# Idle matmuls during the first load, earlier and later places for statistics, more value buffers, and a different end of the program

## The chip, the cores and the metric

The kernel runs on one core of one Trainium2 chip. It is one program and one launch. The metric is the device time of that launch in microseconds, lower is better; a kernel is run several times and the median is given. One further execution is recorded by the hardware profiler; its times are what the profile shows.

## The reference, cut to what matters

Four images of 56 x 56 positions with 256 channels, in f32, pass through four layers. Each layer normalises its input by groups of channels (32 groups of 8, over the whole image), does its own mixing and adds the result to its input:

```python
def _gn(v, G=32, eps=1e-5):
    g = v.reshape(B_, H_, W_, G, C_ // G)
    m = jnp.mean(g, axis=(1, 2, 4), keepdims=True)
    s = jnp.var(g, axis=(1, 2, 4), keepdims=True)
    return ((g - m) / jnp.sqrt(s + eps)).reshape(v.shape)

x = x + L0(_gn(x))   # 7x7 local attention, 8 heads of 32, zero padding
x = x + L1(_gn(x))   # every position against all 3136 of its image
x = x + L2(_gn(x))   # 7x7 neighbourhood attention, 4 heads at dilation 1, 4 at dilation 2
x = x + L3(_gn(x))   # shifted 7x7 windows, 8 heads
```

Layers 0, 2 and 3 are attention: three projections of 256 x 256 to queries, keys and values, logits plus a bias or mask, softmax, the products with the values, and an output projection. Layer 1 normalises rows to unit length, computes exp(5(A - max A)) of all inner products A without the diagonal, divides by the row sums, and applies a 256 x 256 matrix, a norm over channels and a leaky relu to the difference between the row and its weighted mean.

Since the statistics of a group cover a whole image, no row of an image can enter a layer before the last row of that image has left the layer before.

## The kernel before, in words

**Engines.** TensorE (PE) does all products, VectorE (DVE) reciprocals, mask additions and the writing of results with a residual, ScalarE (ACT) exponentials and copies with a bias, GpSimd (POOL) the multiplication of exponentials by masks and the sums of pairs. SyncE (SP) issues nearly all transfers, in one queue of instructions: an issue that has to wait holds up every later one. Each engine runs its instructions in the order in which the program gives them. A planner may choose the order within layers; `issue_after(x)` places what is inside it behind the instruction x in the engine's order. For layer 3 the order is that of the text (`manual_schedule` for PE, DVE, ACT and POOL), for layer 1 that of PE and DVE.

**Layers one after the other.** `direct_blocks` (line 831 on) runs layers 0 to 3. The residual stream goes through DRAM from layer to layer. An image is cut into 7 pieces of 448 positions in layer 0, 8 of 392 in layers 2 and 3. The next layer's first loads and weights are brought in while the layer before ends (`layer2_ahead`, `layer3_ahead`).

**Statistics.** `add_stats` (L896) runs `bn_stats` on DVE for each piece. When the last piece of an image is in, three steps are put into a list `pending`: `channels` (DVE, L910), `mean` (one matmul with a matrix that averages over groups, L914, then ACT, L916 and L917) and `scale` (two matmuls, L921 and L922, then ACT L923 and POOL L924 to L928). `step_stats` takes the next step off the list, `known` takes all that are needed. The matmuls of the steps that run between units write into four spare columns of the bank in which that unit's products lie (`spare`).

**Units.** In layers 0 and 2 the work is a chain of units, each a pair of tiles of queries for 8 heads (`attend_pairs`, L1055 on). For a unit, PE computes the logits (L1080), DVE adds a mask to half of them (L1087), ACT takes exponentials (L1088, L1090), and POOL multiplies the other half by the exponential of the mask (L1091) and adds pairs (`both`, L1102). The products with the values and the row sums (L1113) come one unit later, behind the next unit's logits and a number of "fill" steps (projections of later rows: L952 for queries, keys and outputs, L981 for values). After the products, the unit's list "after" takes steps of statistics, and `done` divides by the row sums (DVE L1272, L1275, L1277 in layer 0; L2008, L2012 in layer 2). In layer 0 a row has four units; `then` (L1329) says which of them take a step of statistics.

**The first image.** Seven pieces are loaded (L1167, order 3, 4, 5, 6, 0, 1, 2); each goes to `bn_stats`; then `known(0, 0)` takes the three steps, ACT normalises (L942), and L981 makes the first values.

**Layer 2.** 16 rows of 8 units (4 images of 4 rows; grids m = 0, 1; pairs i = 0 to 3). Before a unit's logits `gather` (L1990) issues four to eight transfers on SP (L2002), which bring the values of the neighbourhood out of DRAM (`vd`) into a tile `vp2`, of which there are three. `project_out` (L2032) multiplies a finished row by the output weights, adds the residual on DVE (L2044) and stores it. In the last rows `layer3_ahead` is woven in: it loads the first pieces of layer 3, its weights `w_qkv3` in three transfers (L2166) and a mask `m3a` (L2205), normalises two rows, and makes their values.

**Layer 3.** Before its stream of units, layer 3 normalises its third row: `prepare(2)` (L2346), six DVE instructions L945, placed behind `newest[0]`, at that time the last mask addition L1087 of layer 2. The load of the fourth row is issued by `prepare(2)` too.

**The end.** The last row's projection is added to the residual by DVE (`last_row`, L2322) and stored. Throughout, sums which would show an overflow are collected in four tiles `watch`. `unsafe` (L2421) reduces each of them (L2428, four instructions behind `last`, the last addition), compares them to a bound, sums over partitions with a matmul and writes a flag. Every engine loads the flag (L2506) and branches (L2507): if it were set, the whole would be computed again in a slower, safe way (`fused_blocks`); with these inputs it never is, and the branch goes past that code to the closing semaphores and drains.

Of the kernel before, what the change touches and what calls it, by code (L numbers as in the profile page):

```python
# [24 lines left out]
FP = mybir.dt.float32  # L25
# [6 lines left out]
NIMG = 4  # L32
# [798 lines left out]
def direct_blocks(ctx: ExitStack, tc: tile.TileContext, d: dict, watch):  # L831
# [57 lines left out]
    stats, pending, spare = {}, [], []  # L889
# [11 lines left out]
    def group_stats(l, b):  # L901
# [10 lines left out]
        def mean():  # L912
            pm = spare[0](0) if spare else ps_m()
            nc.tensor.matmul(pm[:, :CC], lhsT=group, rhs=mv[:, :, 0], start=True, stop=True)  # L914
# [4 lines left out]
        def scale():  # L919
            pm = spare[0](1) if spare else ps_m()  # L920
            nc.tensor.matmul(pm[:, :CC], lhsT=group, rhs=dv, start=True, stop=False)  # L921
            nc.tensor.matmul(pm[:, :CC], lhsT=group, rhs=mv[:, :, 1], start=False, stop=True)  # L922
# [235 lines left out]
    def layer0(early, big, pool, begin_layer1):  # L1158
# [16 lines left out]
        for r in (3, 4, 5, 6, 0, 1, 2):  # L1175
            load(r, *(() if r < 3 else (looks, "xs")))
            if r < 3:
                add_stats(0, 0, r, xs[r])
            else:
                first_look(r)  # L1180
        known(0, 0)
# [127 lines left out]
        def stream():  # L1309
# [10 lines left out]
            for r in range(NIMG * NB0):  # L1320
# [8 lines left out]
                then = [int(i < 3 and (g > 2 or g == 0)) for i in range(NTC)]  # L1329
# [122 lines left out]
    def layer1(early, big, pool, first, late, next_layer):  # L1452
# [12 lines left out]
        def look_up(q):  # L1465
            if q % 7 == 0:
                rows[:] = [pool.tile([98, 7, NH], FP, tag="rows", name="rows", bufs=1)]
            with tc.issue_after(scaling[-1].ins):
                nc.gpsimd.indirect_dma_start(out=rows[0][:, q % 7, :], out_offset=None, in_=d["table"][:, :],
                                             in_offset=bass.IndirectOffsetOnAxis(ap=idx[:, q:q + 1], axis=0))  # L1470
# [406 lines left out]
    def layer2_ahead(early, held):  # L1877

        xs = held["xs"] = {}

# [17 lines left out]
    def layer2(held, big, pool, last_steps, ends, begin_layer3):  # L1898
# [66 lines left out]
        def pair(r, m, i):  # L1965
# [24 lines left out]
            def gather():  # L1990
                box["o"] = psum_tile("o", 2)
                box["v"] = pool.tile([P, 2, 2, P], FP, tag="vp", name="vp2", bufs=3)
# [41 lines left out]
        def project_out(r):  # L2034
            b, g = divmod(r, NSB)

            def step(y, m, box={}):
# [6 lines left out]
                nc.vector.scalar_tensor_tensor(x[:, m, :], pm, bp2[:, m:m + 1], x[:, m, :], ALU.add, ALU.add)  # L2044
# [99 lines left out]
    def layer3_ahead(big, early, own):  # L2144
# [21 lines left out]
        def load_weight(k):  # L2166
            nc.sync.dma_start(out=w_qkv[:, :, k * C:(k + 1) * C],
                              in_=d["wqkv3"].rearrange("(h p) o -> p h o", p=P)[:, :, k * C:(k + 1) * C])
# [35 lines left out]
        def load_mask():  # L2204
            nc.sync.dma_start(out=m3, in_=m3d[:, 0, :4].rearrange("p h w k -> p h (w k)"))  # L2205

        steps = [lambda: (load(0), load_weight(2)), lambda: load_weight(1),
                 lambda: (prepare(0, later), load_weight(0)), lambda: (prepare(1, later), load_mask())]
        return [transfer, xns, vd, m3, w_qkv, parts, prepare], steps, lazily(values, 0, 3) + lazily(values, 1, 3)

    def layer3(front, pool):
# [152 lines left out]
        u4["done"]()  # L2364
        first()
# [52 lines left out]
    return newest[0].ins  # L2418


def unsafe(tc, pool, watch, flag, last):  # L2421

    nc = tc.nc
    n = len(watch)
    t = pool.tile([P, n + 2], FP, name="bounds")
# [94 lines left out]
```

## Time and profile before

| | us |
|---|---|
| runs shown: median (lowest, highest) of 3 | 3722.86 (3720.98, 3726.05) |
| the profiled execution's own time | 3720.84 |
| its span in the trace | 3719.0 |
| TensorE busy | 3645.2 |
| VectorE busy | 2197.2 |
| GpSimd busy | 1802.9 |
| ScalarE busy | 1479.4 |

The mean granted clock of TensorE is 0.996. In the profile, L12 means line 12 of the kernel; an instruction is written as output tile, line, what it reads and its size; behind it stands the idle time of the engine just before, with the instruction that ended it. A matmul of f32 data appears as two records. Matmuls are pipelined, so busy time counts the engine as taken and not at its peak: at half the clock it is just as busy. In tables of windows there follow, for each stretch, its length, the busy time (and the number of instructions) of PE, weight loads, DVE, ACT and POOL, the granted clock, the busy share of the transfer engines, and GB/s.

### The profile page before, as it was taken

What the parts mean: (1) busy time and instruction counts of PE and PEld (TensorE: products, weight loads), DVE (VectorE), ACT (ScalarE), POOL (GpSimd) and SP (SyncE); (2) the same over time, 40 slices, a digit from 0 to 9 for tenths busy, and PEclk for the clock granted to TensorE, in tenths of its full rate; (3) what the DMA queues carried; (4) which work ended last, traced back from release to release, by engine and by line L of the source; (5) the groups of instructions that cost most, each with busy time, mean ns of one, the idle gap of its engine ahead of it and who ended that gap; (6) DMA issues with size and microseconds to landing.
All of it is one profiled execution on the core that took longest, in us unless ns stands there. A gap on an engine that the chain in (4) does not pass through costs nothing.

```text
span 3719.0 us, 112489 instructions
## 1 busy us (share of the span) xinstructions
PE 3645.2 (98%) x48938; PEld 2480.5 (67%) x48938; DVE 2197.2 (59%) x4176; ACT 1479.4 (40%) x3137; POOL 1802.9 (48%) x1952
## 2 busy tenths in 40 slices
PE   8999999999999999999999999999999999999998
PEld 4666666677776777767777777776666666555554
DVE  5787777544445444554444643445777777677776
ACT  5666665422222222222222222223666666444443
POOL 4777777421235222352222521124877778455555
PEclk9999999999999999999999999999999999999999
DMA  6554444300011000100000000002455444544443
GB/s 223 167 162 138 142 127 139 112 7 24 23 29 33 18 19 19 30 28 23 19 19 23 28 15 11 11 20 78 121 139 145 135 135 127 157 135 133 132 133 100
DMA packets 278695, 304.95 MB, mean 82 GB/s; under 512 B 33670, under 2 KB 269578, under 8 KB 277838
## 3 DMA queue, kind: packets, MB, share of 16 engines
q1 hardware_dynamic: 276336, 297.43, 26.6%
q8 instruction: 386, 6.32, 0.7%
q0 software_dynamic: 1568, 0.16, 0.1%
q14 instruction: 117, 0.96, 0.1%
q10 hardware_dynamic: 288, 0.08, 0.0%
HBM read 205.04 MB, written 92.55 MB: 80 GB/s over the span
## 4 chain that ended last, share of the span: by engine, by line
PE 90%; DVE 4%; POOL 1%; DMA 1%; issue 1%; ACT 1%; SPq 0%; DVEq 0%; ACTq 0%; POOLq 0%
PE ps_m L952 19%; PE ps_o L1683 14%; PE ps_s L1561 14%; PE ps_v L1688 13%; PE ps_m L981 7%; PE ps_o L1113 6%; PE ps_s L1080 6%; PE ps_t L1669 3%; PE ps_o L1040 2%; PE ps_s L1024 1%; PE ps_m L1526 1%; DMA vp<-vd 1%; POOL b L1102 1%; PE ps_m L1418 1%; PE ps_m L1754 1%
## 5 line engine op out<-in xcount | busy, mean ns | idle before, releaser
L1593 DVE TENSOR_TENSOR acc<-acc,ps_v 128x257 f32<-128x257 f32 x1088 | 457.5, 422 | 774.8 <-PE ps_v L1688 751.8
L1688 PE MATMUL ps_v<-xw,e 128*128 128x257 f32 x2208 | 611.1, 381 | 3.5 <-DVE xnT L1538 2.2
L1683 PE MATMUL ps_o<-xw,at 128*128 128x257 f32 x2208 | 609.0, 379 | 0.0
L1561 PE MATMUL ps_s<-xnT,xd 128*128 128x512 f32 (+3 forms) x1344 | 571.4, 548 | 3.9 <-DVE xnT L1538 3.9
L1672 ACT COPY at<-ps_t 128x512 f32<-128x512 f32 (+3 forms) x332 | 170.4, 513 | 953.6 <-PE ps_t L1669 953.4
L1688 PEld LDWEIGHTS ps_v<-xw,e 128*128 128x128 f32 x2208 | 413.4, 189 | 145.0 <-issue 83.2
L1102 POOL TENSOR_TENSOR b<-e 124x448 f32<-124x448 f32 (+5 forms) x498 | 484.7, 994 | 7.2 <-PE ps_o L1113 0.3
L1683 PEld LDWEIGHTS ps_o<-xw,at 128*128 128x128 f32 x2208 | 419.1, 190 | 60.1
L952 PE MATMUL ps_m<-xn,w_wqkv 128*32 128x392 f32 x4096 | 374.3, 494 | 2.3 <-PE ps_s L1080 1.1
L1554 POOL TENSOR_SCALAR xd<-xnT,vec 128x128 f32<-128x128 f32 x192 | 116.1, 614 | 475.6 <-PE ps_s L1561 475.4
L1564 ACT ACTIVATE e<-ps_s 128x512 f32<-128x512 f32 x336 | 185.3, 552 | 354.4 <-PE ps_s L1561 351.1
L1561 PEld LDWEIGHTS ps_s<-xnT,xd 128*128 128x128 f32 x1344 | 225.4, 191 | 141.4 <-issue 126.2
L1091 POOL TENSOR_TENSOR e<-e,m0t 126x672 f32<-126x672 f32 (+3 forms) x128 | 238.7, 1865 | 158.6 <-ACT e L1090 126.2
L1091 POOL TENSOR_TENSOR e<-e,bias 119x784 f32<-119x784 f32 (+5 forms) x128 | 241.7, 1888 | 151.6 <-ACT e L1090 150.8
L1113 PEld LDWEIGHTS ps_o<-e,vp 124*32 124x32 f32 (+3 forms) x8192 | 198.0, 110 | 104.4 <-issue 85.3
L1002 ACT ACTIVATE no<-rs 128x168 f32<-128x168 f32 (+2 forms) x256 | 93.9, 367 | 385.8 <-DVE rs L2008 185.9
L952 PEld LDWEIGHTS ps_m<-xn,w_wqkv 128*32 128x32 f32 x4096 | 124.3, 109 | 176.5 <-issue 128.7
L2008 DVE RECIPROCAL rs<-ps_o 128x196 f32<-128x196 f32 (+2 forms) x128 | 175.7, 1373 | 103.6 <-PE ps_o L1113 83.4
L1113 PE MATMUL ps_o<-e,vp 124*32 124x112 f32 (+3 forms) x8192 | 227.6, 248 | 4.2 <-DMA vp<-vd 3.9
L1088 ACT ACTIVATE e<-e 126x672 f32<-126x672 f32 (+5 forms) x256 | 219.6, 858 | 17.4 <-DVE e L1087 5.0
L1090 ACT ACTIVATE e<-ps_s 126x672 f32<-126x672 f32 (+5 forms) x256 | 206.1, 805 | 8.6 <-PE ps_s L1080 6.4
L981 PE MATMUL ps_m<-w_wqkv,xn 128*32 128x256 f32 x3136 | 197.6, 381 | 3.8 <-DVE xr L2044 2.0
(235 smaller groups left out, 5973.6 us busy)
## 6 DMA issues: line engine op xcount, KB each, us to landing
x<-xr SPq DMA_DIRECT2D x64, 392.0 KB
x<-in_x SPq DMA_DIRECT2D x53, 448.0 KB
x<-x SPq DMA_DIRECT2D x60, 392.0 KB
xr<-x SPq DMA_DIRECT2D x60, 392.0 KB
vd<-v SPq DMA_DIRECT2D x72, 256.0 KB
xr<-in_x SPq DMA_DIRECT2D x32, 392.0 KB
xr<-x SPq DMA_DIRECT2D x28, 448.0 KB
x<-xr SPq DMA_DIRECT2D x28, 448.0 KB
```

The lines of the kernel that those rows point to most:

```text
L952: nc.tensor.matmul(pm[j * HD:(j + 1) * HD, :n], lhsT=w[:, h, col + j * HD:col + (j + 1) * HD], rhs=rhs(h), start=(h == 0), stop=(h == CC - 1))
L981: nc.tensor.matmul(pm[i:i + HD, j * C:(j + 1) * C], lhsT=xn[:, h, first + i:first + i + HD], rhs=w[:, h, :], start=(h == 0), stop=(h == CC ...
L1080: nc.tensor.matmul(s[j // 2][:nk, j % 2, (2 * i + u) * nq:(2 * i + u + 1) * nq], lhsT=k(j, u), rhs=q(j), start=True, stop=True)
L1088: newest.append(nc.scalar.activation(ev, ev, AF.Exp))
L1090: nc.scalar.activation(ev, sv, AF.Exp)
L1091: nc.gpsimd.tensor_tensor(parts(ev), parts(ev), w["emask"], ALU.mult)
L1102: nc.gpsimd.tensor_tensor(w["b"][a][:nk, :, :2 * nq].rearrange("p h (i c) -> p h i c", i=2), ev[:, :, :, 0, :], ev[:, :, :, 1, :], ALU.add)
L1113: nc.tensor.matmul(w["o"](k, i)[j * HD:(j + 1) * HD], lhsT=ones[:nk, :HD] if k else v(j, u), rhs=w["b"][j // 2][:nk, j % 2, i * nq:(i + 1) ...
L1561: nc.tensor.matmul(s[:, :n], lhsT=xd[j][:, h, :], rhs=xnT[:, h, first * P:last * P], start=(h == 0), stop=(h == CC - 1))
L1593: nc.vector.tensor_tensor(acc[:, i, :], acc[:, i, :], pv[:, :C + 1], ALU.add)
L1683: nc.tensor.matmul(out[j][:, :C + 1], lhsT=e[:, col(i)] if i == j else at[:, col(i)], rhs=xw[:, i, :], start=(i == j), stop=(i == NB - 1))
L1688: nc.tensor.matmul(pv[:, :C + 1], lhsT=e[:, col(i)], rhs=xw[:, j, :], start=True, stop=True)
```

## The change

It has five parts.

1. While the pieces of the first image arrive, TensorE multiplies them with an identity matrix, after each load so many times as the tuple (0, 2, 2, 2, 2, 1, 0) says, nine in all, 128 x 448 each; the result is read by nobody. Three more follow the statistics' last matmul. The statistics' steps are placed behind these matmuls in TensorE's order (`grouped`).
2. In layer 0, a row's units 1, 2 and 3 take a step of statistics each, instead of units 0, 1 and 2.
3. In layer 2's last two rows, five units gather their values into tiles of the pool that held layer 2's input pieces ("x", two of them), not into one of the three `vp2`. The three transfers of layer 3's weights become one, and it and the mask are issued by ACT, behind the newest exponential, instead of SP.
4. `newest[0]` becomes the last addition L2044 in the last row of layer 2, so that `prepare(2)` is placed behind it.
5. At the end three of the four reductions of `watch` come before the last row's first half; the fourth stays last, in a block of its own which begins with a hint, on all engines, that the branch over the safe version will be taken. In layer 1, GpSimd executes a drain behind the last of its 49 gathers from a table (L1469).

```diff
+        def busy(x, n):
+            pm = psum_tile("s0", 1, 2)
+            for i in range(n):
+                grouped[:] = [nc.tensor.matmul(pm[:, i % 2, :CH], lhsT=ident, rhs=x[:, i % 2, :], start=True, stop=True)]
+
+        for i, r in enumerate((3, 4, 5, 6, 0, 1, 2)):
             load(r, *(() if r < 3 else (looks, "xs")))
+            busy((xs if r < 3 else looks)[r], (0, 2, 2, 2, 2, 1, 0)[i])
...
-        known(0, 0)
+        for _ in range(3):
+            with tc.issue_after(grouped[0].ins):
+                pending.pop(0)()
+        with tc.issue_after(grouped[0].ins):
+            busy(xs[0], 3)
...
-                then = [int(i < 3 and (g > 2 or g == 0)) for i in range(NTC)]
+                then = [int(i > 0 and (g > 2 or g == 0)) for i in range(NTC)]
...
+            if q == WN - 1:
+                with tc.issue_after(got.ins):
+                    nc.gpsimd.drain()
...
-                box["v"] = pool.tile([P, 2, 2, P], FP, tag="vp", name="vp2", bufs=3)
+                if r < NIMG * NSB - 2 or (8 * r + 2 * i + m) % 5 < 3:
+                    box["v"] = pool.tile([P, 2, 2, P], FP, tag="vp", name="vp2", bufs=3)
+                else:
+                    x = held["pool"].tile([P, CC, WC2], FP, tag="x", name="vx2").rearrange("p h t -> p (h t)")
+                    box["v"] = x[:, :4 * P].rearrange("p (t u e) -> p t u e", t=2, u=2)
...
-                nc.vector.scalar_tensor_tensor(x[:, m, :], pm, bp2[:, m:m + 1], x[:, m, :], ALU.add, ALU.add)
+                added = nc.vector.scalar_tensor_tensor(x[:, m, :], pm, bp2[:, m:m + 1], x[:, m, :], ALU.add, ALU.add)
+                if r == NIMG * NSB - 1:
+                    newest[0] = added
...
-        def load_weight(k):
-            nc.sync.dma_start(out=w_qkv[:, :, k * C:(k + 1) * C],
-                              in_=d["wqkv3"].rearrange("(h p) o -> p h o", p=P)[:, :, k * C:(k + 1) * C])
+        def load_weight():
+            with tc.issue_after(newest[1].ins):
+                nc.scalar.dma_start(out=w_qkv, in_=d["wqkv3"].rearrange("(h p) o -> p h o", p=P))
...
         def load_mask():
-            nc.sync.dma_start(out=m3, in_=m3d[:, 0, :4].rearrange("p h w k -> p h (w k)"))
-
-        steps = [lambda: (load(0), load_weight(2)), lambda: load_weight(1),
-                 lambda: (prepare(0, later), load_weight(0)), lambda: (prepare(1, later), load_mask())]
+            with tc.issue_after(newest[1].ins):
+                nc.scalar.dma_start(out=m3, in_=m3d[:, 0, :4].rearrange("p h w k -> p h (w k)"))
+
+        steps = [lambda: load(0), load_weight, lambda: prepare(0, later), lambda: (prepare(1, later), load_mask())]
...
+        for i in (1, 3, 2):
+            add_up_watch(i)
         first()
         second()
...
-                last = direct_blocks(tc, d, watch)
-                unsafe(tc, wp, watch, flag, last)
+                n = len(watch)
+                bounds = wp.tile([P, n + 2], FP, name="bounds")
+                nc.vector.memset(bounds[:, n + 1:], 1.0)
+
+                def add_up_watch(i):
+                    nc.vector.tensor_reduce(bounds[:, i:i + 1], watch[i], AX.X, ALU.add)
+
+                direct_blocks(tc, d, watch, add_up_watch)
+                with tc.block():
+                    tc.mark_branch_hint_location("again", hint="LikelyTaken", engines=list(mybir.ALL_ENGINES))
+                    add_up_watch(0)
+                    unsafe(tc, bounds, n, flag)
             again = nc.values_load(flag)
-            with tc.If(again > 0):
+            with tc.If(again > 0, label="again"):
                 fused_blocks(tc, d)
```

More of the change, by code (lines that the diff above doesn't have):

```diff
@@ L830, in direct_blocks @@
 @with_exitstack
-def direct_blocks(ctx: ExitStack, tc: tile.TileContext, d: dict, watch):
+def direct_blocks(ctx: ExitStack, tc: tile.TileContext, d: dict, watch, add_up_watch):
     nc = tc.nc
@@ L888, in direct_blocks @@
     raw = [[const.tile([P, CC, n, 6], FP, name=f"st{l}_{b}") for b in range(NIMG)] for l, n in enumerate(parts_of)]
-    stats, pending, spare = {}, [], []
+    stats, pending, spare, grouped = {}, [], [], []
     seen_parts = {}
@@ L913, in mean @@
             pm = spare[0](0) if spare else ps_m()
-            nc.tensor.matmul(pm[:, :CC], lhsT=group, rhs=mv[:, :, 0], start=True, stop=True)
+            grouped[:] = [nc.tensor.matmul(pm[:, :CC], lhsT=group, rhs=mv[:, :, 0], start=True, stop=True)]
             for h in range(CC):
@@ L921, in scale @@
             nc.tensor.matmul(pm[:, :CC], lhsT=group, rhs=dv, start=True, stop=False)
-            nc.tensor.matmul(pm[:, :CC], lhsT=group, rhs=mv[:, :, 1], start=False, stop=True)
+            grouped[:] = [nc.tensor.matmul(pm[:, :CC], lhsT=group, rhs=mv[:, :, 1], start=False, stop=True)]
             nc.scalar.activation(dv, pm[:, :CC], AF.Identity, bias=gn_eps)
@@ L1174, in layer0 @@
         q = {(0, i): early.tile([P, CC, BT], FP, tag="q", name="q0", bufs=6) for i in range(3)}
-        for r in (3, 4, 5, 6, 0, 1, 2):
+        def busy(x, n):
[3 more added lines that the diff above has]
+        for i, r in enumerate((3, 4, 5, 6, 0, 1, 2)):
             load(r, *(() if r < 3 else (looks, "xs")))
+            busy((xs if r < 3 else looks)[r], (0, 2, 2, 2, 2, 1, 0)[i])
             if r < 3:
@@ L1468, in look_up @@
             with tc.issue_after(scaling[-1].ins):
-                nc.gpsimd.indirect_dma_start(out=rows[0][:, q % 7, :], out_offset=None, in_=d["table"][:, :],
-                                             in_offset=bass.IndirectOffsetOnAxis(ap=idx[:, q:q + 1], axis=0))
+                got = nc.gpsimd.indirect_dma_start(out=rows[0][:, q % 7, :], out_offset=None, in_=d["table"][:, :],
+                                                   in_offset=bass.IndirectOffsetOnAxis(ap=idx[:, q:q + 1], axis=0))
+            if q == WN - 1:
+                with tc.issue_after(got.ins):
+                    nc.gpsimd.drain()
             if q % 7 == 6:
@@ L1879, in layer2_ahead @@
         xs = held["xs"] = {}
+        held["pool"] = early
         def load(i):
@@ L2417, in direct_blocks, with unsafe @@
     fronts.close()
-    return newest[0].ins
-def unsafe(tc, pool, watch, flag, last):
+def unsafe(tc, t, n, flag):
     nc = tc.nc
-    n = len(watch)
-    t = pool.tile([P, n + 2], FP, name="bounds")
-    for i, w in enumerate(watch):
-        with tc.issue_after(last):
-            nc.vector.tensor_reduce(t[:, i:i + 1], w, AX.X, ALU.add)
     nc.vector.tensor_tensor(t[:, :n], t[:, :n], t[:, :n], ALU.mult)
@@ L2431, in unsafe @@
     nc.vector.tensor_reduce(t[:, n:n + 1], t[:, :n], AX.X, ALU.min)
-    nc.vector.memset(t[:, n + 1:], 1.0)
     with tc.tile_pool(name="psum_end", bufs=1, space=PSUM) as ps:
```

## The prediction

> **What bounds the kernel now.** I read the busy table and the chain first, then asked where TensorE's remainder lies.
>
> ```profile
> PE 3645.2 (98%) x48938; PEld 2480.5 (67%) x48938; DVE 2197.2 (59%) x4176; ACT 1479.4 (40%) x3137; POOL 1802.9 (48%) x1952
> PE 90%; DVE 4%; POOL 1%; DMA 1%; issue 1%; ACT 1%; SPq 0%; DVEq 0%; ACTq 0%; POOLq 0%
> ```
>
> TensorE is busy for 3645.2 of 3719.0 us. The change removes no matmul of the computation, so it can only fill the 74 us left over, or turn half-clock time, which counts as busy, into full-clock time. The timeline of the start shows the first place:
>
> ```profile
> 4.89 1.15 DVE L896 BATCH_NORM_STATS2 st<-x 128x6 f32<-128x448 f32 x2 [0.62 <-DMA x<-in_x]
> 13.98 0.59 PE L914 MATMUL ps_m<-mv,group 128*128 128x2 f32 x2 [13.98 <-DVE mv L910]
> 18.71 5.35 PE L981 MATMUL ps_m<-w_wv,xn 128*32 128x256 f32 x48 [2.62 <-ACT xn L942]
> ```
>
> TensorE waits 13.98 us for seven loads and the statistics on DVE. The 48 matmuls of L981 then take 5.35 us; the same 48 take 2.6 us late in the run (379 ns each instead of 634). So the start runs at half clock, although the granted-clock column, which has its first record at 24.67, cannot say so.
>
> The waits of TensorE, asked stretch by stretch (us in total, times, longest), show three more places: layer 0 (127 to 135 us), the end of layer 2 (3143 to 3200), and the passage to layer 3 (3200 to 3215).
>
> ```profile
> PE ps_m L952 <- DVE attn L1277: 0.8, 1, 0.8
> ...
> PE ps_o L1113 <- DMA vp<-vd: 3.6, 6, 1.0
> ...
> PE ps_m L981 <- DVE xr L2044: 2.0, 1, 2.0
> ```
>
> Each of the latter two is followed by half clock. In the windows below, read the first pair (TensorE's busy time) and the sixth figure (granted clock):
>
> ```profile
> 3171.77:3175.18 3.41, 1.56 (x36) 0.68 (x28) 2.11 (x4) 2.02 (x4) 3.41 (x4) 1.00 0.55 181
> 3175.18:3178.59 3.41, 3.14 (x60) 2.48 (x58) 1.30 (x1) 0.00 (x0) 1.17 (x1) 0.50 0.42 140
> 3202.49:3205.90 3.41, 1.37 (x40) 0.94 (x40) 3.41 (x7) 0.00 (x0) 0.93 (x1) 1.00 0.12 45
> 3205.90:3209.31 3.41, 3.41 (x68) 2.50 (x60) 2.96 (x6) 0.44 (x2) 0.00 (x0) 0.50 0.59 195
> ```
>
> Last, the end. DVE's flag is done at 3709.57, the span ends at 3719.0: 9.5 us in which no engine computes. The sequencers' records there: loads of the flag to 3710.1, compare-and-branch to 3710.29, nothing on any engine until 3713.8 to 3714.35, SP's row of semaphores to 3715.45, GpSimd's DRAIN 3714.14 to 3718.21 (4069 ns; its other three drains take 172, 106 and 40 ns), a barrier of 0.84.
>
> **Part by part.**
>
> *A, multiplications during the load.* Nine 128x448 matmuls enter before L914, three after L922. No row has them; the nearest is L1561 (512 columns, 571.4 us / 1344 = 425 ns per record, two records each), so 0.74 us warm and 1.49 cold. The first has its image rows at about 6.2. Records of the clock lie on a grid of 3.413 us through 24.67, so the first wholly busy window would be 7.60 to 11.02. Until 11.02 3.2 are done, the other 5.8 take 4.3: L914 starts at 15.3 instead of 13.98, 1.3 late (1.49 us each throughout would end at 19.6, 5.6 late). The three statistics matmuls, warm (0.38 against 0.59 for L914; 0.61 against 1.02 for L921 with L922), return 0.6. The three later ones take 2.2 us and lie inside the 2.6 us wait for ACT's normalisation. L981 then saves 2.7. Net with the clock up: 2.0; if the half clock returns before L981, a loss of 0.7. [...] the row 13.98 says that the warm-up itself stands in the queue ahead of L914. I take 1.0, between, range -1.8 to +2.7.
>
> *B, statistics in layer 0.* Steps that fell on a row's first unit now fall on the unit before it in TensorE's order (L914 or L921/L922 one unit or one row earlier). At 285.3 ACT's L916/L917 read the bank which DVE's L1272 wants (1.24 us wait), the mask addition L1087 goes ahead of L1277, and L952 waits: 0.77 at 130.33, 0.97 at 288.89, 0.97 at 447.98, sum 2.7. A longer wait at 622.52 (0.88) stays. Nothing becomes later. DVE's 0.53 for L910 lies behind a unit of matmuls. 2.7 (1.5 to 3).
>
> *C, value buffers.* In rows 14 and 15 five units (m is the grid, i the pair) use tiles left free by the loads, so their gathers L2002 need not wait until a buffer of three is read; three loads of weights (0.64, 0.71, 0.47) and the mask (0.45) leave SP, 2.27 us, with the lane waits behind them:
>
> ```profile
> SPq L2041 <- DMA x<-xr: 1.5, 1, 1.5
> SPq L2002 <- DMA m3a<-m3d: 1.1, 1, 1.1
> ```
>
> Units take 3.52 us undisturbed; three of them in 3161 to 3184 take 2.2, 3.05 and 2.9 more: 8.2 us, of which 3.56 are the waits above and 3.4 the half clock of 3175.18 to 3182.00 (6.8 / 2); the rest is pauses between. SP issues 4 to 8 gathers of 0.73 us per unit, and GpSimd's multiplications and sums (L1091, L1102) stand behind as the next bound:
>
> ```profile
> 3143.00:3161.00 18.00, 17.69 (x468) 12.09 (x462) 15.34 (x21) 10.63 (x24) 16.01 (x14) 1.00 0.48 144
> 3161.00:3184.00 23.00, 19.33 (x468) 12.76 (x456) 15.08 (x22) 13.67 (x31) 16.43 (x14) 0.85 0.65 194
> ```
>
> In the second row (busy us of TensorE, its weight loads, DVE, ACT, GpSimd) GpSimd has 16.43 us to do, TensorE 19.33 less 3.4 of half clock, 15.9. So the 23.0 us can't fall under 16.4: at most 6.6 there. I take 6.0 (2 to 8, since work of the stretch before may come forward). The two loads on ACT cost it an issue each (0.43 and 0.48 for its two at the start) plus at most the 1.1 of lane wait; behind them stand L1002, L1090 and L1088 of the next unit, for which L1091 and then TensorE wait. ACT is busy 10.63 of 18 us: that idle time hides it; if it is gone, 1 to 2 us.
>
> *D, normalisation of layer 3's third row.* Six DVE L945 stand before the last L2044:
>
> ```profile
> 3201.36 2.68 DVE xn L945 x4
> 3204.04 0.54 DVE xr L2044
> 3204.62 1.07 PE ps_m L981 x16
> ```
>
> Behind the last L2044 they no longer hold TensorE: 2.04 of wait, 1.7 of half clock. DVE then has the reciprocals of the last two units (about 1.4 each), which hold L952 in any case: 2.6 (1 to 3.7). What is late next: xn of row 2, done near 3215.5 and read at 3223; and load of row 3 (issued at 3208.2 before), some 7 us later on SP ahead of the mask m3c and the projection weight, which are not read before 3226.
>
> *E, the end.* Three of four L2428 move into DVE's 1.04 us idle before L2322: 0.5. The hint: [...] 0.05 to 0.08 for the branch, 3.55 to 4.1 until the next instruction. [...] By the rows, a fetch begun behind DVE's last addition (3707.39) ends 4.1 later at 3711.5, where DVE now resumes at 3714.35: 2.85 off for the latest engine, more for the others. I go by the rows. The drain in layer 1: GpSimd's last gather there is at 1927.12, and it idles 2.27 us before 1931.76; 4.1 us there delay L1566 by 1.7 at most and are spent before ACT and TensorE need it. Whether it takes the later 4.07 away depends on what that waits for; the only long drain is the one after gathers by software queue, so I expect yes. Both working: DVE resumes at 3711.5, SP's row, then waiting for DVE alone, ends 0.35 later, the barrier adds 0.85, end 3712.7, 6.3 off; I take 6.0. Hint alone: GpSimd's drain starts at 3709.8 and holds the end at 3714.8, 4.2 off. Drain alone: 3714.35 less 0.5, plus 1.1 of SP's row and 0.85, 3715.8, 3.2 off. Neither: 0.5.
>
> Sum: 1.0 + 2.7 + 6.0 + 2.6 + 6.0 = 18.3 off the execution's own 3720.84 (span 3719.0): 3702.5. The median of the runs shown is 2.0 above that execution, so 3704.6.
>
> **The rivals.** *The drain takes nothing* (GpSimd still stalls 4.07): 1.8 back, 3706.4. For it: a drain of 40 ns comes after the long one, so it isn't fixed; against: 1790 us pass after the last gather without clearing it. *The hint doesn't act* (wrong block, or the fetch isn't begun): 2.8 back, 3707.4; with the drain as well 3710.1. That is the change not doing what it says. *SP and GpSimd keep the gathers and the e tiles late*: C gives 2, 3708.6; for it stand 16.01 of 18 us. *The nine matmuls delay the statistics*: A gives -1.8, 3707.4; for it stand the 13.98 and their place in the queue. *Slower*: the two ACT loads. By the semaphores of the trace SP and ACT share eight lanes, each load waiting for the eighth before it; if ACT's issue waits for a gather that itself waits for a buffer, its exponentials stand, and each TensorE stall costs its length plus up to 3.4 of half clock. It decides only above 25.8 us (18.3 plus 7.45), six stalls of 0.9 with their half clock; against it, the longest lane wait of this stretch is 1.5. That would give 3731.
>
> **How the numbers follow.** 0.2% is 7.45 us, about what a measurement of this kernel can tell from no change: below 3715.4 is faster, above 3730.3 slower. Forecast with its bounds 0.48; drain alone failing 0.18; hint failing 0.12; gathers late 0.09; statistics late 0.05; several of these and small misses together, around 3717, 0.05; slower 0.03. Range: A to D at the upper ends of their gains are 5.1 below the forecast and the lowest run of before 1.9 below its median, which gives 3698; above, hint and drain both failing (3710.1) and 1.9 more of A or D, 3712. Chances: faster 0.92, same 0.05, slower 0.03.
>
> **What would show it.** A: L981 x48 near 2.6 us, beginning by 19.5. B: no wait on L1277 at 130, 289, 448. C: no half clock in 3160 to 3185, waits on vp under 1 us; wrong if GpSimd's b or SP's lanes stand in their place. D: L981 of row 1 follows L2044 without 2 us of idle. E: first instructions after the branch by 3.0 us sooner, GpSimd's DRAIN at the end under 0.2 us and one of about 4 in layer 1. It is wrong if half clock appears where none was, or if TensorE waits for exponentials from ACT near 3150.

## The result, and the profile after

The changed kernel takes 3713.99 us, the median of 22 runs (3706.57 to 3722.41); the kernel before 3718.73 (22 runs, 3714.01 to 3726.05). The ratio is 0.9987, with a 95% interval of 0.9981 to 0.9993: 4.8 us faster, 2.6 to 7.1, where 18.3 were forecast. The absolute forecast of 3704.6 was built on a median of three runs, 3722.86, which lay 4.1 above the median of more runs, so a gain of 18.3 would have given 3700.4.

The profiled executions alone would mislead. They differ by 14.2 us of span (3719.0 and 3704.8), three times the difference of the medians. The first two lines of the page of after:

```profile
PE 3645.5 (98%) x48962; PEld 2478.3 (67%) x48962; DVE 2197.2 (59%) x4176; ACT 1478.8 (40%) x3137; POOL 1804.2 (49%) x1952
PE 89%; DVE 5%; POOL 2%; ACT 1%; DMA 1%; issue 1%; SPq 0%; DVEq 0%; ACTq 0%; POOLq 0%
```

TensorE has 24 records more (the twelve idle matmuls) and nearly the same busy time, 98%. At the start, in the timeline of TensorE, the first nine idle matmuls hold the engine until 16.4, so that L914 begins 2.4 us later than before; the other three (L1179 below) follow the statistics, and L981 x48 takes 3.02 us instead of 5.35:

```profile
16.40 0.28 PE L914 MATMUL ps_m<-mv,group 128*128 128x2 f32 x2
17.65 2.50 PE L1179 MATMUL ps_s<-x,ident 128*128 128x448 f32 x6
20.42 3.02 PE L981 MATMUL ps_m<-w_wv,xn 128*32 128x256 f32 x48 [0.27 <-ACT xn L942]
```

The three waits of layer 0 on the division by the row sums are gone, but near 130 us a wait of the same length on a copy by ACT (L1236) has come for the first of them. Three more new waits stand in the views of after by stretch: one of DVE and, behind it, of TensorE near 617 us; one on ACT's exponential where the gathers' waits were; one on the values of layer 3 near 3220 (us in total, times, longest).

```profile
PE ps_m L952 <- ACT kE L1236: 0.8, 1, 0.8
...
DVE attn L1288 <- DMA vd<-v: 2.2, 1, 2.2
...
PE ps_s L1080 <- DVE e L1087: 2.2, 1, 2.2
...
PE ps_s L1080 <- ACT e L1090: 1.7, 1, 1.7
...
PE ps_o L1040 <- DMA v<-vd: 0.8, 1, 0.8
```

Near 617 us TensorE waited 0.3 us in the kernel before; the wait of after is followed by a stretch at half clock (the figure 0.50):

```profile
PE ps_s L1080 <- DVE e L1087: 0.3, 1, 0.3
```
```profile
615.00:618.16 3.16, 0.96 (x44) 0.72 (x32) 1.46 (x4) 0.94 (x3) 2.08 (x1) 1.00 0.62 151
618.16:621.57 3.41, 3.41 (x42) 2.28 (x46) 2.88 (x4) 2.39 (x5) 2.48 (x3) 0.50 1.01 314
```

And the end. Before, all four reductions stood behind the last additions; in after, three lie ahead of them, as forecast, and the flag is done at 3697.87.

```profile
3706.70 0.69 DVE L2322 TENSOR_TENSOR xr<-xr,ps_s 128x343 f32<-128x343 f32 x3
3707.31 1.14 DVE L2428 TENSOR_REDUCE bounds<-watch 128x1 f32<-128x392 f32 x4
```

```profile
3693.80 0.67 DVE L2525 TENSOR_REDUCE bounds<-watch 128x1 f32<-128x6 f32 x3
3694.93 0.69 DVE L2343 TENSOR_TENSOR xr<-xr,ps_o 128x343 f32<-128x343 f32 x3 [0.46 <-PE ps_o L2336]
...
3697.73 0.14 DVE L2452 TENSOR_SCALAR flag<-n_safe 1x1 int32<-1x1 f32 x1 [0.37 <-PE n_safe L2451]
```

From there to the end of the span are 6.9 us instead of 9.5. The records of the sequencers say which part of it went (us):

```
                         before            after
compare-and-branch, ACT  3710.13-3710.18   3698.45-3698.52
next instruction, ACT    3714.01 (3.83)    3702.48 (3.97)
GpSimd's DRAIN           4.069             0.056
hint, ACT                none              3692.97
DRAIN in layer 1         none              ends 1926.09, 4.07 behind the last gather
```

The drain is moved away at no visible cost; the hint has no visible effect.

### The profile page after: what moved, and what is told of

It reads as the page before. It is cut to its first block, busy times and chain, and to the rows that moved or that the text cites. A ratio compares the mean times of both kernels' runs of the same rounds, so it can differ in the third digit from the quotient of the medians.

```text
span 3704.8 us, 112537 instructions
## 1 busy us (share of the span) xinstructions
PE 3645.5 (98%) x48962; PEld 2478.3 (67%) x48962; DVE 2197.2 (59%) x4176; ACT 1478.8 (40%) x3137; POOL 1804.2 (49%) x1952
## 4 chain that ended last, share of the span: by engine, by line
PE 89%; DVE 5%; POOL 2%; ACT 1%; DMA 1%; issue 1%; SPq 0%; DVEq 0%; ACTq 0%; POOLq 0%
PE ps_m L952 18%; PE ps_o L1697 14%; PE ps_s L1575 14%; PE ps_v L1702 13%; PE ps_m L981 6%; PE ps_o L1113 6%; PE ps_s L1080 5%; PE ps_t L1683 3%; PE ps_o L1040 2%; PE ps_s L1024 1%; PE ps_m L1540 1%; POOL b L1102 1%; DVE e L1087 1%; DVE rs L1286 1%; DVE st L896 1%
## 5 line engine op out<-in xcount | busy, mean ns | idle before, releaser
L952 PE MATMUL ps_m<-xn,w_wqkv 128*32 128x392 f32 x4096 | 374.3, 494 | 1.2 <-ACT xn L942 0.9
L1113 PEld LDWEIGHTS ps_o<-e,vp 124*32 124x32 f32 (+5 forms) x8000 | 192.7, 110 | 97.0 <-issue 82.1
L1002 ACT ACTIVATE no<-rs 128x168 f32<-128x168 f32 (+2 forms) x256 | 93.9, 367 | 385.3 <-DVE rs L2027 174.1
L952 PEld LDWEIGHTS ps_m<-xn,w_wqkv 128*32 128x32 f32 x4096 | 124.1, 109 | 175.8 <-issue 127.7
L1113 PE MATMUL ps_o<-e,vp 124*32 124x112 f32 (+5 forms) x8000 | 220.3, 248 | 0.3
L1090 ACT ACTIVATE e<-ps_s 126x672 f32<-126x672 f32 (+5 forms) x256 | 206.2, 806 | 3.8 <-PE ps_s L1080 3.8
L981 PE MATMUL ps_m<-w_wqkv,xn 128*32 128x256 f32 x3136 | 197.4, 381 | 1.8 <-DVE v L987 1.6
```

The source lines that it names most:

```text
L952: nc.tensor.matmul(pm[j * HD:(j + 1) * HD, :n], lhsT=w[:, h, col + j * HD:col + (j + 1) * HD], rhs=rhs(h), start=(h == 0), stop=(h == CC - 1))
L981: nc.tensor.matmul(pm[i:i + HD, j * C:(j + 1) * C], lhsT=xn[:, h, first + i:first + i + HD], rhs=w[:, h, :], start=(h == 0), stop=(h == CC ...
L1090: nc.scalar.activation(ev, sv, AF.Exp)
L1113: nc.tensor.matmul(w["o"](k, i)[j * HD:(j + 1) * HD], lhsT=ones[:nk, :HD] if k else v(j, u), rhs=w["b"][j // 2][:nk, j % 2, i * nq:(i + 1) ...
```

## The experiments

All ratios are to the kernel before, with 95% intervals. Since a single profile had just misled, the first pair asks how far two profiles of one program agree.

**Both kernels once more, unchanged.**

> The kernel before, unchanged, as a yardstick and for a second trace of it. Theory 1 (the half-clock windows follow the phase of a free-running 3.413 us grid, which differs in each execution): ratio 1.000 with an interval of about 0.001; the same waits at the same places as in the first trace (2.04 us on L2044, 3.6 us on vp, 2.7 us on L1277 in layer 0), but the half-clock windows at other places or in another number than six. Theory 2 (the half-clock windows belong to fixed places of the program): half clock again at 639, 666, 683, 3175 and 3206 us, 24 us in all.

> The changed kernel, unchanged, for a second trace. Theory 1: its first profiled execution (3706.57, one half-clock window) was a lucky one out of 22 with a median of 3713.99; this one shows three to eight half-clock windows, a span of 3709 to 3716, the same waits elsewhere, and the difference in span to the first trace is half of the difference in half-clock time. Theory 2: one half-clock window again and a span of 3703 to 3707, so that the profiled path is representative and the 22 runs differ from it for another reason.

Measured: before again 0.9993 (0.9985 to 1.0001), after again 0.9986 (0.9979 to 0.9992), the latter with a span of 3712.7. Windows of the second trace of after (length; busy time of TensorE, its weight loads, DVE, ACT, GpSimd; granted clock; share and rate of transfers):

```profile
616.79:620.20 3.41, 1.86 (x42) 1.34 (x46) 3.34 (x5) 1.77 (x4) 2.42 (x3) 1.00 0.97 312
620.20:623.61 3.41, 3.41 (x52) 2.10 (x48) 1.47 (x3) 1.05 (x2) 3.33 (x4) 0.50 1.01 304
633.86:637.27 3.41, 2.13 (x34) 1.79 (x38) 2.47 (x4) 2.33 (x4) 3.41 (x4) 1.00 0.62 177
637.27:644.10 6.83, 6.83 (x76) 5.69 (x65) 3.10 (x4) 3.09 (x6) 6.83 (x7) 0.50 0.16 50
664.58:667.99 3.41, 3.41 (x46) 2.92 (x46) 1.39 (x3) 0.95 (x1) 3.13 (x3) 0.50 0.14 37
3163.13:3166.54 3.41, 3.41 (x44) 1.86 (x40) 0.98 (x1) 3.38 (x11) 3.07 (x3) 0.50 0.93 337
```

The less of a grid window TensorE is busy, the more often the next one is at half clock. Counted over all windows at full clock in the 14 traces of this document: where TensorE was busy for less than 1.6 us of 3.4, 18 of 20 were followed by half clock; from 1.6 to 2.0 us, 21 of 32; from 2.0 to 2.6 us, 21 of 174; from 2.6 us on, none. By these counts it matters how much of a pause falls into one window, and so where the window's edges fall. Half-clock time before the end of the program, by trace:

| kernel | half clock, us |
|---|---|
| before, two traces | 23.9, 20.5 |
| after, two traces | 3.4, 23.9 |
| the other ten kernels below | 10.2 to 27.3 |

So the first trace of after, 3.4 us, was a lucky execution: of the 14.2 us between the first two traces up to 10 are, by an estimate from the granted clock of 0.50, half of this difference in half-clock time (20.5 / 2). Theory 1 holds for the number. It does not hold in full for the places: in the kernels before, half clock fell in both traces near 638, 665, 682 and 3174; only the one near 3206 was absent in the second. Theory 2's fixed places are nearer to the truth there than I allowed: these weak spots drew half clock in both executions, that one in one of two.

**The hint without a branch between it and its own.** In the change, the hint's block is left by an unconditional branch ahead of the conditional one; the trace of after has no record of it.

```diff
-            with tc.tile_pool(name="watch", bufs=1) as wp:
+            watching = ExitStack()
+            wp = watching.enter_context(tc.tile_pool(name="watch", bufs=1))
...
-                    unsafe(tc, bounds, n, flag)
-            again = nc.values_load(flag)
-            with tc.If(again > 0, label="again"):
-                fused_blocks(tc, d)
+                    unsafe(tc, bounds, n, flag)
+                    watching.close()
+                    again = nc.values_load(flag)
+                    with tc.If(again > 0, label="again"):
+                        fused_blocks(tc, d)
```

> The changed kernel with the flag's load and the branch inside the hint's own block, so that no other branch stands between the hint and the branch it is meant for. Theory 1 (the unconditional branch between them uses the hint up): the first instruction behind the branch comes within 1 to 2 us instead of 3.97, the fetch of instructions begins before the branch, and the time falls by 2 to 3 us, ratio to before about 0.998. Theory 2 (the hint has no effect here at all): 3.9 to 4.0 us again, fetch beginning about 0.9 us behind the branch, time as the changed kernel's.

Measured: 0.9983 (0.9975 to 0.9991), not separable from the changed kernel. ACT's hint is executed at 3697.81, its branch ends at 3703.37, its next instruction comes at 3707.02, 3.65 later (3.97 and 3.77 in the two traces of after, 3.83 and 3.56 before without a hint). The packets of the second instruction queue begin at 3704.26, 0.9 behind the branch, as in after (3699.39 behind 3698.52) and in before, without a hint (3711.06 behind 3710.18). Theory 1 falls: the hint has no visible effect in either place. Why it has none stays open.

**The branch by itself.**

```diff
-            again = nc.values_load(flag)
-            with tc.If(again > 0, label="again"):
-                fused_blocks(tc, d)
+            nc.values_load(flag)
```

> The changed kernel without the flag's load, the branch, the hint and the safe version behind it, to measure the price of the branch by itself; the outputs are computed as before. Theory (the 3.6 to 4.0 us behind the branch are the fetch of instructions far away): the closing semaphores follow the flag within 0.5 us instead of 4.6 to 4.9, the end lies about 4.3 us (with the flag's load) nearer. If the gap stays, it is not the branch's.

Measured: 0.9974 (0.9967 to 0.9981), 4.5 us less than after again by the ratios. (The load, whose value nothing uses any more, leaves no record in the trace.) The closing semaphores begin 0.03 us behind the flag, the end comes 2.4 us behind it instead of 6.8. So the price was rightly read: load, branch and what follows it until the next instruction cost some 4.4 us. How much of that a hint could save isn't shown.

**The drain alone, in the kernel before.**

```diff
+            if q == WN - 1:
+                with tc.issue_after(got.ins):
+                    nc.gpsimd.drain()
```

> The kernel before with one addition, GpSimd's drain behind the last gather from the table in layer 1. Theory (the drain at the end waits for what the gathers by software queue left, and whoever drains first pays it): GpSimd's drain in layer 1 takes 4 us, that at the end under 0.1 instead of 4.07, and the span from the flag to the end falls from 9.4 to 6.8 or 6.9 us, no wait of TensorE appears near it. Rival (it is the reductions or the hint that shortened the end): 4.07 us at the end again.

Measured: 0.9994 (0.9985 to 1.0003); the time alone doesn't decide. The trace does: in layer 1 GpSimd is held from the gather's end at 1927.29 to 1931.35, 4.06 us, TensorE waits for nothing between 1920 and 1940, GpSimd's drain at the end takes 0.056, and the way from flag to end is 5.9 us instead of 9.5 and 9.4, a little shorter than expected because SP came back from the branch after 3.04. The drain takes its 4 us at its first execution behind the gathers, not at the end.

**Without the idle matmuls, and the idle matmuls alone.**

```diff
-            busy((xs if r < 3 else looks)[r], (0, 2, 2, 2, 2, 1, 0)[i])
...
-        for _ in range(3):
-            with tc.issue_after(grouped[0].ins):
-                pending.pop(0)()
-        with tc.issue_after(grouped[0].ins):
-            busy(xs[0], 3)
+        known(0, 0)
```

> The changed kernel without the twelve idle matmuls (part A undone). If they bring what the first trace showed, the first keys' matmul L952 begins about 0.6 us later and the span is 0.9 longer beyond the half-clock windows (24.0 us at the first L952 instead of 23.4); if they cost (rival: statistics late), the start is shorter without them.

Measured: 0.9981 (0.9973 to 0.9989), a median of 3709.53 beside 3712.78 of the changed kernel on the same chip. The ratios' intervals overlap; the means of the two kernels' own runs (13 and 21) differ by 2.4 us, with a 95% interval of 0.7 to 4.1. Its first L952 stands at 23.73, after's two at 23.39 and 22.85, so the start is longer without them, as the first theory said. But two views of the stretch 612 to 624 have changed, TensorE's and DVE's:

```profile
PE ps_s L1080 <- DVE e L1087: 0.7, 1, 0.7
...
DVE attn L1283 <- DMA vd<-v: 0.7, 1, 0.7
```

The wait near 617 is a third of what it was. To see whether it belongs to the idle matmuls, they alone were put into the kernel before:

> The kernel before with the twelve idle matmuls alone (part A alone). Theory (they bring a little at the start, dependent on the phase of the clock's grid, and put a store of values late near 617 us): from the end of L910 to the first L1080 24.7 to 26.2 us, on the line of the other kernels that have them (25.1 where the first full-clock record is at 9.8, 26.0 where it is at 11.8), against 25.8 to 26.1 before; DVE waits 2 to 3 us for the store of values near 617 and L1080 behind it, against 0.4 and less before; the time is not below that of before, ratio 0.9995 to 1.0010. Rival (the late store comes from another part, and the idle matmuls only bring their gain at the start): wait near 617 at 0.4 or less, ratio 0.9995 or lower.

Measured: 1.0006 (0.9999 to 1.0012), 3719.46 against 3717.84: no faster, and at most a little slower. Waits of TensorE and of DVE from 612 to 624:

```profile
PE ps_s L1080 <- DVE e L1087: 2.3, 1, 2.3
...
DVE attn L1287 <- DMA vd<-v: 2.3, 1, 2.3
```

The wait is theirs: it comes with them alone, and without them it is 0.7 or less. In all nine traces of kernels that have the idle matmuls L1080 waits 2.1 to 3.4 us here; in the five without, 0.1 (three times), 0.3 and 0.7. In seven of the nine, 3.4 or 6.8 us at half clock begin between 617 and 623 us; in none of the five. The runs say the same: the mean granted clock is 0.9958 with the idle matmuls alone and 0.9967 before (21 and 25 runs, a difference of 0.0009 with a 95% interval of 0.0005 to 0.0013); it is 0.9974 without them and 0.9963 in the changed kernel (13 and 21 runs). The idle matmuls, which were to raise the clock, lower it over the whole run.

Why the wait comes is shown in part only. SP's order of transfers in layer 0's first rows differs between the two groups; here it is the same, but the load xr<-in_x is issued 2.5 us behind the begin of L981 instead of 1.3, just ahead of the stores vd<-v, and DVE goes on 3.7 us behind the end of the second store's issue (after) instead of 2.5 (before). Which of the earlier shifts made it late isn't shown.

The gain at the start, from the end of L910 to the first L1080, against the first record of full clock:

| kernels | first full-clock record, us | end of L910 to first L1080, us |
|---|---|---|
| without (5 traces) | 21.6 to 24.7 | 25.3 to 26.1, mean 25.7 |
| with: after again, hint nested, loads on SP | 9.2, 9.5, 9.8 | 24.8, 24.9, 25.1 |
| with: idle alone, no D, after | 10.2, 10.2, 10.6 | 25.2, 25.1, 25.4 |
| with: no extra buffers, no B, no fallback | 11.7, 11.8, 12.1 | 25.8, 26.0, 26.2 |

The mean with them is 25.4: 0.4 us gained (25.74 less 25.37), from 1.0 down to a loss of 0.5: by the table the less, the later the first record of full clock.

**The two loads on SP again.**

```diff
-            with tc.issue_after(newest[1].ins):
-                nc.scalar.dma_start(out=w_qkv, in_=d["wqkv3"].rearrange("(h p) o -> p h o", p=P))
+            nc.sync.dma_start(out=w_qkv, in_=d["wqkv3"].rearrange("(h p) o -> p h o", p=P))
...
-            with tc.issue_after(newest[1].ins):
-                nc.scalar.dma_start(out=m3, in_=m3d[:, 0, :4].rearrange("p h w k -> p h (w k)"))
+            nc.sync.dma_start(out=m3, in_=m3d[:, 0, :4].rearrange("p h w k -> p h (w k)"))
```

> The changed kernel with the weights of layer 3 (one load) and the mask issued by SP again, the extra value buffers kept. Theory (ACT stands in front of these loads until their lane is free, and the exponentials behind it hold TensorE): the wait of L1080 on ACT's L1090 between 3155 and 3180 us, 1.7 us in the first trace of the changed kernel, 5.5 in the second, falls to nothing; the stretch from 3140 to 3215 us is 2 to 5 us shorter than in the changed kernel, half-clock windows apart. Rival (the gathers are late anyway, since SP is the bound): waits of L1113 on vp come back, 2 us or more in sum, and the stretch is no shorter. Time: ratio to before 0.998 or, by the rival, as the changed kernel's 0.9986.

Measured: 0.9976 (0.9968 to 0.9984), 3710.55; by time alone not separable from the changed kernel, whose interval reaches down to 0.9979. The traces decide. First what ACT does in the second trace of after, from its waits and its timeline:

```profile
ACT no L1002 <- DMA vp<-vd: 6.8, 1, 6.8
```
```profile
3153.12 0.81 ACT L1090 ACTIVATE e<-ps_s 119x784 f32<-119x784 f32 x1
3161.15 0.40 ACTq L2189 DMA_DIRECT2D w_wqkv<-in_wqkv  x1
3162.04 0.71 ACT L1090 ACTIVATE e<-ps_s 126x672 f32<-126x672 f32 x1
```

ACT is done with an exponential at 3154.83 and stands until 3161.15 in front of the load, whose lane is taken by a gather vp<-vd. (A lane is one of the eight semaphores on which the transfers of SP and ACT report that they have landed. In the trace of before 1665 transfers, two of them ACT's, take them in turn without an exception; in the first trace of after the load of the weights is issued at 3153.70, 0.02 us behind the last record, at 3153.68, of the semaphore of a gather that SP issued at 3150.43, and the mask at 3163.88, 0.02 behind that of a load issued at 3160.60.) SP issues the gather for which ACT stands only at 3158.43, 3.6 us after ACT was ready, when it has worked through the transfers ahead of it. L1002 and the next unit's L1090 are queued behind the load and begin at 3161.65 and 3162.04. TensorE waits for that L1090. The waits of TensorE from 3143 to 3200, in the second trace of after, then with the loads on SP:

```profile
PE ps_s L1080 <- ACT e L1090: 5.5, 2, 3.5
PE ps_o L1113 <- POOL b L1102: 1.0, 2, 0.7
```
```profile
PE ps_o L1113 <- POOL b L1102: 2.2, 4, 0.7
```

With the loads on SP there is neither a wait on ACT nor one on vp; only GpSimd's sums remain. The stretch from 3140 to 3215 is 7.5 us shorter than in the first trace of before, against 5.2 and 1.2 in the traces of after, and it holds no half clock. The rival falls: SP isn't the bound once the buffers are there.

**The loads on ACT, without the extra buffers.**

```diff
-                if r < NIMG * NSB - 2 or (8 * r + 2 * i + m) % 5 < 3:
+                if True:
```

> The changed kernel with all value gathers in the three buffers again, the two loads still on ACT. Theory (ACT's stand in front of the loads is the new wait, whatever the buffers): a wait of L1080 on ACT's L1090 of 1 us or more remains, and waits on vp of 1 to 3.6 us return. Rival (the early gathers fill the lanes and so cause ACT's wait): the wait on ACT's L1090 is gone, and only waits on vp are left.

Measured: 0.9988 (0.9981 to 0.9995). The waits of TensorE from 3143 to 3200:

```profile
PE ps_s L1080 <- ACT e L1090: 4.0, 1, 4.0
...
PE ps_o L1113 <- DMA vp<-vd: 0.5, 1, 0.5
```

The wait is there without the buffers: the loads on ACT make it. Waits on vp hardly return, 0.5 instead of the 1 or more expected; that ACT's stand delays what would have waited for them is likely, not shown.

**B undone, and D undone.**

```diff
-                then = [int(i > 0 and (g > 2 or g == 0)) for i in range(NTC)]
+                then = [int(i < 3 and (g > 2 or g == 0)) for i in range(NTC)]
```

> The changed kernel with the statistics of layer 0 on units 0 to 2 again (part B undone). The three waits of L952 on L1277's counterpart return (0.77, 0.97, 0.97 us near 128, 286 and 445). If part B also caused the new wait of L1080 on DVE's L1087 near 617 us (2.1 to 2.2 us; 0.35 and below 0.15 before), it falls to 0.4 or less; if it comes from elsewhere, it stays near 2.1, or at the 0.7 which it is without the idle matmuls.

Measured: 0.9993 (0.9984 to 1.0002). Waits of TensorE in 120 to 135, in 284 to 291 and in 440 to 450, and last in 612 to 624:

```profile
PE ps_m L952 <- DVE attn L1288: 0.8, 1, 0.8
...
PE ps_m L952 <- DVE attn L1288: 1.0, 1, 1.0
...
PE ps_m L952 <- DVE attn L1288: 1.0, 1, 1.0
...
PE ps_s L1080 <- DVE e L1087: 2.4, 1, 2.4
```

B is worth its 2.7 us: from 110 to 470 us the first trace of after gains 2.8 on before, this kernel 0.0. The gain isn't spread as forecast: 0.1 from 110 to 132, where the wait on L1236 has come, 1.3 from 284 to 291, 1.0 from 440 to 452, and 0.4 between. And the wait near 617 stays, so it isn't B's.

```diff
-                if r == NIMG * NSB - 1:
-                    newest[0] = added
```

> The changed kernel with the third row of layer 3 normalised before the last additions of layer 2 again (part D undone). The wait of L981 on the addition of the residual returns (1.7 to 2.0 us near 3200), the waits of L1040 on the values' transfer near 3220 (0.8 to 1.1 us, not there before) go. Net about 1 us longer in the stretch 3195 to 3240, half-clock windows apart.

Measured: 0.9990 (0.9981 to 1.0000). Waits of TensorE from 3200 to 3240:

```profile
PE ps_m L981 <- DVE xr L2063: 2.0, 1, 2.0
PE ps_m L952 <- DVE attn L2031: 0.9, 1, 0.9
```

The 2.0 us are back, and L1040 waits for v no more. From 3195 to 3240 this kernel gains 0.6 on before, the two traces of after 2.2 and 1.9: D is worth 1.3 to 1.5 by these. The wait for v varies: over the nine traces of kernels with D it is 0.5 to 4.0 us, in the five without there is none. Where it was longest, in the traces of the nested hint (1.7) and of the last kernel below (4.0), half clock followed and the stretch is 0.4 and 3.8 longer than in before.

**What pays, together.** No idle matmuls, the loads on SP, no hint; B, the buffers, D, the reductions and the drain stay. The three edits are those shown, and the hint's block goes:

```diff
-                with tc.block():
-                    tc.mark_branch_hint_location("again", hint="LikelyTaken", engines=list(mybir.ALL_ENGINES))
-                    add_up_watch(0)
-                    unsafe(tc, bounds, n, flag)
+                add_up_watch(0)
+                unsafe(tc, bounds, n, flag)
```

> The changed kernel with three things taken back: no idle matmuls, the two loads of layer 3 issued by SP, no branch hint. What stays is the statistics a step elsewhere in layer 0, the value buffers, the third row's normalisation behind the last addition, the reductions' place and the drain. Theory (the idle matmuls bring 0.8 us at the start and cost 1.5 to 2.3 near 617; the loads on ACT cost 1.7 to 5.5; the hint does nothing): no wait of L1080 on ACT's L1090 in 3150 to 3180, the wait near 617 at 0.7 or less, 3.6 to 4.0 us from the branch to the next instruction as with the hint; a median near 3708, ratio to before 0.9972 (0.9964 to 0.9980). Rival (the idle matmuls help after all, through the clock): a ratio no better than the 0.9976 of the kernel that has only the loads back on SP.

Measured: 3706.67, 0.9973 (0.9963 to 0.9983), faster than both kernels by the medians; against the changed kernel (0.9986 and 0.9987) it lies 1.3 thousandths lower, with intervals that overlap by 0.0004 and 0.0002. From the 0.9976 of the kernel that keeps the idle matmuls the runs don't separate it, so the rival isn't excluded by time. The waits near 617 and on ACT are gone; the branch costs 3.5 us (ACT) without a hint. Its profiled execution was its slowest of nine (3714.23), with a wait for v of 4.0 us near 3220 and half clock behind it. Its waits from 3143 to 3200:

```profile
PE ps_o L1113 <- POOL b L1102: 1.7, 3, 0.7
PE ps_o L1113 <- issue: 1.1, 1, 1.1
PE ps_m L952 <- DVE attn L2026: 0.6, 1, 0.6
```

None is on ACT or on vp. From flag to end it takes 6.9 us, as with the hint. The mean granted clock of its nine runs is 0.9979, of the 37 of before on this chip 0.9968: 0.0011 more, with a 95% interval of 0.0006 to 0.0017.

## Why the prediction was wrong

Its direction held (faster), its size did not: 18.3 forecast, 4.8 measured. By its own steps, where "shown" is read from waits and stretches of the traces:

| step | forecast | shown |
|---|---|---|
| A, start | 1.0 | 0.4 in the mean (1.0 to -0.5) |
| A, elsewhere | 0 | -2.0 near 617, half clock behind it not counted |
| B | 2.7 | 2.7 to 2.8 |
| C, waits | 2.6 | 3.6 on vp gone, 1.7 to 5.5 on ACT come (mean of seven traces 3.3): about 0 |
| D, waits | 0.9 | 2.0 gone, 0.8 and 1.1 on v come in the two traces of after: about 1.1 |
| half clock in C and D | 5.1 | none in the mean |
| E, reductions and drain | 3.2 | 3.1 |
| E, hint | 2.8 | 0 |
| sum | 18.3 | about 5 |

The sum of what is shown, 0.4 - 2.0 + 2.7 + 0 + 1.1 + 3.1 = 5.3, fits the 4.8 of the runs, with half clock taken as equal on both sides. That is what the runs' mean granted clocks say, 0.9966 before (163 runs) and 0.9964 after (43 runs); by the prediction it should have risen. That the sum fits so well is in part luck, since single traces of a kernel differ by more than a term of it.

*The step that failed first* is in C: "ACT is busy 10.63 of 18 us: that idle time hides it; if it is gone, 1 to 2 us." A mean over 18 us says nothing on an instruction that waits in order. I had priced the wait by the 1.1 us that SP's gather stood behind the mask. On ACT it is 1.9 to 6.8 us, since the lane is held by an earlier transfer that hasn't landed, in the longest case a gather which SP had not even issued when ACT was ready, and every exponential stands behind it. The prediction's own sign of being wrong, TensorE waiting for exponentials from ACT near 3150, came, at 3166 us in the first trace of after, at 3163 and 3174 in the second. The rival "slower: the two ACT loads" had the mechanism exactly (an issue that waits for a lane, exponentials behind it), but I asked only whether it would turn the whole change slower (six stalls) and gave it 0.03. It took half of what C saves in waits in the first trace of after (1.7 of 3.6) and more than all of it in the second (5.5).

*The second* is the half clock counted as belonging to the waits: "3.4 the half clock of 3175.18 to 3182.00" and "1.7 of half clock". Where the waits really go, with the loads on SP, half clock in 3160 to 3215 goes too. In the second trace of the changed kernel new waits took the old ones' place and drew it again, and a second trace of before had 6.8 us there instead of 10.2. One trace shows one phase of the grid (the first full-clock record is at 24.67 and 23.11 us in the two of before); A's range, -1.8 to 2.7, was my estimate of what the phase can do at the start; I did not apply it to these places. So the 5.1 us failed for the changed kernel, not as such: without the idle matmuls and with the loads on SP the granted clock does rise, by 0.0011, and at the 3 us per 0.001 read below that is an estimated 3.4 us. The idle matmuls alone lowered it by 0.0009.

*The third* is the hint: "a fetch begun behind DVE's last addition (3707.39) ends 4.1 later". The price of the branch was right (4.5 us with the load of the flag, by the kernel without it); that the hint begins a fetch was assumed, and no row showed one: in before the packets of the second instruction queue begin at 3711.06, 0.88 behind the branch of ACT, and in after, with the hint 5.5 us ahead, 0.87 behind it. (The branch itself takes 0.05 to 0.09 us on four engines.) The rival "the hint doesn't act" had it: 2.8 forecast, and from flag to end 6.9 us where drain and hint together should have given 3.6.

*The fourth* is "A": L914 came 2.4 us late where 1.3 were worked out, although the clock was up at 10.59, earlier than assumed. That the first wholly busy window brings it up was my assumption; in after full clock is recorded behind a window with TensorE busy for 3.35 of 3.41 us (7.18 to 10.59), in before behind one with 3.41 (21.26 to 24.67) and not behind the one ahead of it, with 2.55. The time of the idle matmuls was taken too short: at full clock a record of theirs took 0.42 (six in 2.50 us) to 0.47 (ten in 4.67), where 0.37 was scaled by columns from L1561. The gain of 2.7 at L981 was 2.3; the late L981 that it was read from takes 2.8 us for its 48 by its own row, not 2.6. And nothing in the working looked for the effect far away, which cost more than the start gained; the new wait near 617 has no row in before but a small one, the 0.3 us there.

*Right*: B's sum to a tenth, which is partly luck, since the first of its three waits was replaced by another and part of the gain came from stretches that were not counted; D's 2.0 us; the reductions' 0.5; the drain, with the rival against it (1790 us without clearing) refuted; xn of row 2 in time. Of "what is late next" for D, the load of row 3 was named, and the values' gather of layer 3, which is what waits now, was not followed. A slip without weight: the edit gives six units, not five, a tile of the freed pool (24 gathers vx<-vd, four a unit).

## What to carry to other kernels

Before a transfer is moved to an engine that also computes, ask not how busy the engine is, but how long the issue may stand (here 1.9 to 6.8 us on an engine that was busy for 10.63 of 18): which earlier transfer holds its lane, and which instructions are queued behind. Half-clock time seen in one trace is no sum to be saved (3.4 and 23.9 us in two of one kernel): take a second trace, and compare the mean granted clock of many runs. Work that is added to fill a pause can move transfers far behind it (the idle matmuls of the first 20 us went with a wait of 2.1 to 3.4 us near 617): look for new waits over the whole span, not only where it was added. A large difference between two profiles needs the medians beside it before it is explained.

## What the runs showed of the hardware

GpSimd's DRAIN took 4.06 to 4.07 us at its first execution behind the gathers from the table, whether 1790 us later (4.069, before) or at once (4.06 and 4.07 in layer 1, counted from the last gather's end; its record there begins before that gather and is 6.76 long), and 0.056 at its next. Moved to layer 1 (the kernel with the drain alone), it cost TensorE no wait from 1920 to 1940 us.

The branch over the safe version cost 2.9 to 4.4 us until the next instruction, on every engine in the 13 traces that have it, with a hint up to 5.5 us ahead or without.

A window of 3.413 us at half clock followed most windows in which TensorE was busy for less than 2.0 us (39 of 52) and none in which it was busy for 2.6 or more.

The same program's executions differ by up to 16 us (3706.57 to 3722.41), and most of that goes with half-clock time: in the 22 runs of after the time falls by about 3 us for each 0.001 of mean granted clock (correlation -0.84).
